# Five buffers of relus in place of six and twelve blocks in place of eleven, in a fused attention and expert layer

## The chip, the cores and the metric

The kernel runs on one core of a Trainium2 chip. Its engines are TensorE (PE: matmuls, with PEld for its weight loads), VectorE (DVE), ScalarE (ACT), GpSimd (POOL) and SyncE (SP, which here only starts DMAs). The metric is the device time of one execution in microseconds (us).

## What is computed

A layer over x of shape (4, 1024, 128): a normalisation, then power-law attention with 16 heads of width 8 and a mixture of 8 experts, of which each token uses two. The sum of both is added to x. All of it is in 32-bit floats.

```python
xn = _layernorm(x)
# attention, per head
q, k, v = split(xn @ W_attn + b_attn)
s = einsum('bhtd,bhsd->bhts', q, k)
s = s - s.mean(-1)
mad = abs(s).mean(-1) + 1e-06            # over all keys, before the causal mask
s = s / mad * score_gain
r = maximum(where(causal, s, -1000), 0) ** 4
y = (r / (r.sum(-1) + 1e-06)) @ v        # then @ W_proj + b_proj
# experts: top 2 of 8 by xn @ gate_w + gate_b, softmax over the two
h = (xn @ w1 + b1) * (xn @ w2 + b2)
e = silu(h @ wg + bg) @ w3 + b3
out = x + attention + sum of weighted e
```

## The kernel before

**Attention.** For each of the four batches, `prepare` makes queries, keys and values. The keys are written four times, each time masked to the heads of one of four groups (`keys`, L908), so that a matmul on 32 of PE's rows yields one head's scores, and four such matmuls run side by side. Queries, masked keys, transposed rows and normalised rows each lie in a buffer of kind `blk`.

`chunk` handles 512 queries of a batch; there are two chunks in a batch, four head groups r in a chunk. Two streams of steps run through it:

- "up" (L1010): scores of all keys, for the mean of their absolute values; ACT (L1025) or DVE (L1023) drains them.
- "score" (L1134): causal scores, keys on the partitions. A group is four heads by up to 512 queries, in four PSUM banks. DVE masks the diagonal part (L1153), and ACT (L1160) or DVE (L1162) takes the relu of the rest; both write two buffers of kind `u1`. Then ACT (L1185) or POOL (L1187) squares `u1` into a buffer of kind `u`, and squares `u` in place. The fourth powers times the values (L1210, `values`) and the plain relus times a constant (L1201, `relus`: the sum of absolute values that the relu gives) are added up in one PSUM bank.

There are 160 such groups. `flush` puts the values of one group and the relu sums of the next into one PE step, L1210 followed by L1201. At the end of a head group, `finish` turns the result and normalises it (L1078 to L1099); at the end of a chunk it is projected (L1267, L1269).

**Experts.** `route` finds places for the tokens; POOL scatters the rows to memory with 64 indirect DMAs (L776), from where 36 expert steps, each of two tiles of 128 rows, read them (L1303), with their weights (L1311 to L1314, eight DMAs a step on SP). Their matmuls are L1342, L1351 and L1360; POOL adds the results into memory with indirect DMAs (L1380).

**Order.** Nothing is ordered by hand. Each step is a `Node` with the engines that may do it, their durations, the nodes that it depends on, the buffers that it takes and gives back, and a rank. `Plan.run` goes through them once, at build time: again and again it takes the node whose start, less a lead from the table `SOONER`, is earliest, breaks ties by the rank (with an offset from the table `RANK`), puts it on that engine, and lets its buffers go or come free at planned times; `HOP` is the planned delay from a step's end to what depends on it. The program is issued in that order, so each engine's queue is fixed. On the chip an engine waits only for what its data and buffers need.

The buffers are counted in `kinds` (L245 to L253): 8 PSUM banks, 8 of `u`, 6 of `u1`, 11 of `blk`. A score takes four banks and two `u1`. A pair of `u1` is given back by a "free" node, which has no instruction:

```python
relu_job = dict(..., free=(u1s, e2), ...)          # L1219: e2, the second squares
...
add("free", {"none": 0.0}, None, deps=[n] + e2, give=u1s)   # L1063: n, the flush with the relu sums
```

A buffer of `u1` has 4096 bytes in each partition, one of `blk` 4160. PE also gets filler matmuls in planned gaps (L1531, L1536).

Of the kernel before, what the change touches and what calls it, by code (L numbers as in the profile page):

```python
# [16 lines left out]
P = 128  # L17
# [6 lines left out]
CH = 512  # L24
# [28 lines left out]
class Plan:  # L53

    HOP = 0.12
    LAG = {"PE": 0.2, "DVE": 0.085, "ACT": 0.1, "POOL": 0.045}

    SOONER = {"score": 0.46, "sum": -0.74, "mean": 0.17, "wT@DVE": 0.13, "norm@ACT": -0.05, "place": 0.03, "sums": 0.22, "relu0": -0.21, "relu2": -0.08, "score0": 0.74, "score2": 0.58, "sq2": 0.1, "ys0": -0.42, "out": -0.17, "v": -0.03, "gain": -0.81, "absq": 0.38, "abs0": -0.55, "sq0": -0.35, "proj": -0.44, "xT": 0.07, "second": -0.98, "up2": 0.18, "yT": 0.14, "up": 0.32, "sq@ACT": -0.27, "tbias": -0.01, "mask0": 0.04, "up0": 0.3, "abs0@DVE": 0.57, "ys2": -0.14, "ys@DVE": -0.79, "sq@POOL": -0.64, "weight": -0.19, "gate@ACT": -0.71, "count": 0.31, "k": 0.27, "turn": -0.06, "xT@ACT": 0.41, "y@DVE": 0.14, "gateT": 0.32, "abs2@DVE": 0.08, "gate": 0.05, "scatter": -0.07, "heads@ACT": 0.06, "abs@DVE": -0.3, "exp": 0.12, "xT@DVE": -0.16, "moments": -0.1, "keys": -0.69, "heads@DVE": 0.12, "relu0@ACT": -0.27, "rows": -0.52, "av0": -0.04, "scale": 0.09, "sq2@ACT": -0.42, "xg": -0.43, "av2": 0.03, "ys": 0.07, "abs2": 0.05, "warm": -0.75, "bias": -0.8, "gates": 0.91, "std": 0.14, "ys@ACT": -0.12, "sq0@ACT": -0.2, "q@ACT": 0.05, "ys2@ACT": -0.68, "mask": -0.04, "q": 0.08, "bound@DVE": -0.04, "norm": 0.17, "y": 0.11, "yT@DVE": -0.66, "norm@DVE": -0.66, "ys0@ACT": 0.07, "give": 0.2, "sq0@POOL": 0.01, "yT@ACT": -0.42, "headsT": 0.91, "abs2@ACT": -0.01, "blocks": -0.07, "sq": -0.1, "rows_in": -0.92, "xg@ACT": 0.35, "h": 0.17, "relu@DVE": -0.2, "load": 0.26, "xg@DVE": -0.07, "bound": 0.03, "abs": 0.51, "spill": -0.52, "kappa": 0.65, "relu2@DVE": -0.07, "relu": 0.05}  # L60
    RANK = {"xg": -16, "headsT": 6, "spill": 168, "blocks": 174, "wT": 8, "absq": 58, "abs": 20, "weight": 101, "gain": 188, "keys": -227, "abs2": 39, "sq2": 19, "ys0": -9, "up0": -37, "score2": 1, "av": -8, "second": 1, "score0": 14, "relu2": 94, "heads": -7, "norm": 28, "abs0": -107, "h": 174, "sums": 228, "av0": 17, "xT": -7, "relu": -11, "stats": -9, "rows_in": -149, "gateT": -21, "sq": 161, "top": 102, "reload": 84, "ys2": 27, "k": 242, "up": 10, "hot": -130, "score": -18, "sum": 13, "mean": 156, "kappa": -33, "load": -208, "warm": 37, "ys": -195, "yT": 1, "turn": -123, "rows": -17, "av2": 1, "out": 6, "normal": 62, "proj": -184, "scale": 29, "fill": 13, "mask2": 35, "sq0": -53, "tbias": -32, "count": 13, "gates": 7, "std": 24, "up2": -6, "gate": 6, "bias": 6, "mask0": -13, "v": 14, "scatter": 1, "g": 53, "moments": -184}
    MODE = {"up": "rows", "score": "rows", "av": "columns", "gate": "columns", "heads": "columns"}

    @classmethod
# [113 lines left out]
def layer_kernel(  # L178
# [44 lines left out]
    TB = T // P  # L223
# [8 lines left out]
    WX = C + 2  # L232
# [9 lines left out]
    def keep(shape, name, dtype=F32):  # L242
# [2 lines left out]

    kinds = {
        "bank": (8, [P, CH]),
        "u": (8, [P, 2, CH]), "u1": (6, [P, 2, CH]), "blk": (11, [P, TB * WX]),
        "w": (4, [P, 2 * F + FB * F + FB * C]), "xg": (3, [P, SB, WX]), "xT": (2, [P, TW]),
        "z": (2, [P, FB, TW]), "s": (2, [P, FB, TW]), "ye": (2, [P, SB, C]),         "ys": (2, [P, CH]), "yt": (2, [P, CB, C]),  # L250
        "yT": (1, [P, CH]), "wT": (2, [P, P]), "asum": (2, [P, 2, CB, NH]), "shead": (2, [P, TB, NH]),
# [8 lines left out]
    add = plan.add  # L260
# [11 lines left out]
    rows = keep([3, P], "rows")  # L272
# [8 lines left out]
    gain = keep([P, 1], "gain")  # L281
# [14 lines left out]
    for r in range(NR):  # L296
        for g in range(4):
            h = g * NR + r
# [20 lines left out]
    for base, step in ((0, -D), (D - 1, D)):  # L319
        nc.gpsimd.affine_select(  # L320
            out=same.rearrange("p (h d) -> p h d", d=D), in_=same.rearrange("p (h d) -> p h d", d=D),
# [7 lines left out]
        out=causal[:, : 2 * P].rearrange("p (n k) -> p n k", k=P), in_=causal[:, : 2 * P].rearrange("p (n k) -> p n k", k=P),  # L329
# [3 lines left out]
    for i in range(kinds["V"][0]):  # L333
        v = keep([P, TB, VW], f"V_{i}")
# [11 lines left out]
        out=behind_, in_=behind_, compare_op=ALU.is_ge, fill=0.0,  # L346
# [53 lines left out]
    none = tiles["w"][0][:, FILL * WX : FILL * WX + 2 * C]  # L400
# [43 lines left out]
    hot = [keep([P, E, NTB], f"hot_{k}") for k in range(2)]  # L444
# [350 lines left out]
    q, km, Vb, sh, prepared, keyed = {}, {}, {}, {}, {}, {}  # L795
# [190 lines left out]
    def chunk(b, c, vd, sh_done, t0, t1):  # L986
# [10 lines left out]
        for n, (r, unit) in enumerate(work):  # L997
# [20 lines left out]
            for g, k in enumerate(ks_):  # L1018
                def drain(e, r=r, parts=parts, g=g, k=k):
                    for i, sg, _, w, at in parts:  # L1020
# [9 lines left out]
                        deps=[a], behind=drained[0][:1], take=[] if drained[0] else [asum], give=[k], rank=rank - 200,  # L1030
# [15 lines left out]
        def flush(jobs, rank):  # L1046

            n = add(
                "av" + stage, {"PE": sum(o["took"] for o in jobs)}, lambda e: [o["emit"](e) for o in jobs],
                deps=[d for o in jobs for d in o["deps"]] + chain, take=[t for o in jobs for t in o["take"]],  # L1050
                give=[u for o in jobs for u in o["give"]], rank=rank - 20,
                behind=line["turn"][-2:-1] if any(o["take"] for o in jobs) else [],
            )
            chain[:] = [n]
            for o in jobs:
                if o["last"]:
                    n.closed = o["acc"]
                else:
                    n.open = o["acc"]
            for o in jobs:  # L1060
                if o["free"]:
                    u1s, e2 = o["free"]
                    add("free", {"none": 0.0}, None, deps=[n] + e2, give=u1s)  # L1063
                if o["last"]:
                    finish(*o["last"], n, rank)

# [46 lines left out]
        for r in range(NR):  # L1113
            acc = Buf("bank")
            for j, grp in enumerate(groups):
                diag = grp[0][0] >= c * CB
# [9 lines left out]
                e1, e2, sq1 = [], [], []  # L1126
                u1s, us = ([Buf(kind) for _ in range(2)] for kind in ("u1", "u"))
# [17 lines left out]
                for m in range(2):  # L1145
                    u1, u = u1s[m], us[m]
# [59 lines left out]
                def values(e, r=r, parts=parts, us=us, acc=acc, begin=False, end=False):  # L1206
# [362 lines left out]
```

## Time and profile before

| | us |
|---|---|
| median of 3 runs | 919.82 |
| lowest, highest | 916.57, 923.04 |
| profiled execution | 898.9 |
| its span, first to last instruction | 897.2 |
| granted TensorE clock, mean | 0.993 |

A table of busy time lists for each engine how long it was at work. A line of the groups names the line of the kernel, the engine, the operation, output and input, the count and the mean time of one. PE's matmuls overlap, so the time of a group of them is that of their union.

```profile
L1187 POOL TENSOR_TENSOR u<-u 128x1024 f32<-128x1024 f32 (+1 forms) x302 | 523.7, 1828 | 97.6 <-ACT u L1160 50.3
L1185 ACT ACTIVATE u<-u 128x1024 f32<-128x1024 f32 (+1 forms) x338 | 324.9, 991 | 7.0 <-DVE u L1162 3.1
L1025 ACT ACTIVATE bank<-bank 128x512 f32<-128x512 f32 (+3 forms) x351 | 170.6, 487 | 33.6 <-PE bank L1010 30.7
L1160 ACT ACTIVATE u<-bank 128x256 f32<-128x256 f32 (+2 forms) x353 | 152.9, 496 | 35.1 <-PE bank L1134 17.8
```

The 640 squares are shared by POOL (302, 1.83 us each on average) and ACT (338, 0.99 us). The last part of a line is the idle time of the engine just before such instructions, and what ended most of it: POOL stood idle for 97.6 us before squares, 50.3 us of it until ACT had written relus.

### The profile page before, as it was taken

The numbers are of one execution on the slowest core, as the hardware profiler recorded it, in microseconds if no ns is written. First come the engines' busy times: TensorE is split into PE (matmuls) and PEld (weight loads), VectorE is DVE, ScalarE is ACT, GpSimd is POOL, SyncE is SP. The second block draws the span as 40 slices with busy tenths as digits, with TensorE's granted clock in tenths as the row PEclk, the third lists the DMA queues.
The fourth block names the chain that finished last, engine by engine and source line by source line (L and its number), as shares of the span: only waits on it lengthen the run. The fifth ranks groups of instructions, "written<-read, shape, count | busy, mean of one in ns | idle before, by whom it ended". The sixth has DMA issues, their size and how long they took to land.

```text
span 897.2 us, 22584 instructions
## 1 busy us (share of the span) xinstructions
PE 878.7 (98%) x8067; PEld 472.7 (53%) x8067; DVE 592.8 (66%) x1557; ACT 787.4 (88%) x1881; POOL 709.8 (79%) x563
## 2 busy tenths in 40 slices
PE   7899999999999999999999999999999999999997
PEld 6455533334545555555566665555545666544444
DVE  6988967677875655655666576555756775755555
ACT  4978999999997999899988989989988978889995
POOL 4368999999996869787667839889787567599998
PEclk9989999999999999999999999999999999999999
DMA  4753000000001443535444534354213444422115
GB/s 112 289 160 100 25 26 28 32 16 25 23 22 35 108 130 85 134 74 138 99 107 108 136 85 129 85 132 116 71 49 75 103 107 107 111 72 53 24 14 187
DMA packets 92318, 79.20 MB, mean 88 GB/s; under 512 B 8431, under 2 KB 88366, under 8 KB 92206
## 3 DMA queue, kind: packets, MB, share of 16 engines
q1 hardware_dynamic: 79064, 68.50, 25.5%
q0 software_dynamic: 12416, 8.99, 7.1%
q8 instruction: 64, 1.05, 0.5%
q10 hardware_dynamic: 726, 0.27, 0.2%
q14 instruction: 48, 0.39, 0.1%
HBM read 58.13 MB, written 19.60 MB: 87 GB/s over the span
## 4 chain that ended last, share of the span: by engine, by line
PE 83%; ACT 6%; DVE 4%; POOL 4%; issue 2%; DMA 0%; ACTq 0%; DVEq 0%; POOLq 0%
PE bank L1010 16%; PE bank L1134 15%; PE bank L1210 14%; PE bank L1201 10%; PE bank L1351 7%; PE bank L1342 7%; PE bank L1360 4%; POOL u L1187 2%; ACT u L1185 2%; POOL xs L776 2%; PE bank L1078 1%; ACT u L1160 1%; PE bank L1531 1%; DVE asum L1023 1%; PE bank L826 1%
## 5 line engine op out<-in xcount | busy, mean ns | idle before, releaser
L1187 POOL TENSOR_TENSOR u<-u 128x1024 f32<-128x1024 f32 (+1 forms) x302 | 523.7, 1828 | 97.6 <-ACT u L1160 50.3
L1185 ACT ACTIVATE u<-u 128x1024 f32<-128x1024 f32 (+1 forms) x338 | 324.9, 991 | 7.0 <-DVE u L1162 3.1
L1023 DVE TENSOR_REDUCE asum<-bank 128x1 f32<-128x512 f32 (+3 forms) x417 | 203.1, 547 | 71.2 <-PE bank L1010 70.1
L1025 ACT ACTIVATE bank<-bank 128x512 f32<-128x512 f32 (+3 forms) x351 | 170.6, 487 | 33.6 <-PE bank L1010 30.7
L1160 ACT ACTIVATE u<-bank 128x256 f32<-128x256 f32 (+2 forms) x353 | 152.9, 496 | 35.1 <-PE bank L1134 17.8
L1010 PE MATMUL bank<-blk,blk 32*128 32x512 f32 (+3 forms) x1536 | 181.0, 523 | 1.6 <-ACT s L1452 1.5
L1134 PE MATMUL bank<-blk,blk 32*128 32x512 f32 (+3 forms) x1536 | 179.2, 529 | 1.2 <-ACT blk L908 0.7
L1153 DVE SCALAR_TENSOR_TENSOR u<-bank,causal 128x256 f32<-128x256 f32 (+1 forms) x384 | 121.2, 373 | 75.9 <-PE bank L1134 39.2
L1380 POOL DMA_INDIRECT acc<-ye,xg x72 | 113.4, 1574 | 66.5 <-DVE ye L1372 40.1
L1210 PE MATMUL bank<-u,V 128*32 128x512 f32 (+3 forms) x1536 | 159.5, 498 | 0.0
L1162 DVE TENSOR_SCALAR u<-bank 128x512 f32<-128x512 f32 (+1 forms) x159 | 99.3, 660 | 50.1 <-PE bank L1134 50.0
L1010 PEld LDWEIGHTS bank<-blk,blk 32*128 32x128 f32 x1536 | 87.3, 184 | 78.9 <-DVE asum L1023 14.8
L1201 PE MATMUL bank<-u,pick 128*32 128x512 f32 (+3 forms) x1280 | 125.4, 469 | 0.0
L1134 PEld LDWEIGHTS bank<-blk,blk 32*128 32x128 f32 x1536 | 65.9, 185 | 65.1 <-issue 26.1
L1201 PEld LDWEIGHTS bank<-u,pick 128*32 128x32 f32 x1280 | 42.2, 111 | 80.2 <-issue 75.6
L1210 PEld LDWEIGHTS bank<-u,V 128*32 128x32 f32 x1536 | 32.8, 108 | 88.3 <-issue 66.6
L1351 PEld LDWEIGHTS bank<-z,w 128*128 128x128 f32 x576 | 67.2, 192 | 18.4 <-issue 5.9
L1426 DVE SCALAR_TENSOR_TENSOR z<-bank,biases,z 128x128 f32<-128x128 f32 x144 | 43.6, 345 | 46.2 <-ACT z L1419 45.3
L1351 PE MATMUL bank<-z,w 128*128 128x128 f32 x576 | 73.3, 280 | 0.0
L776 POOL DMA_INDIRECT xs<-blk,slot x64 | 62.7, 979 | 13.5 <-issue 11.2
L1342 PE MATMUL bank<-xT,w 128*128 128x128 f32 x576 | 70.3, 275 | 0.0
L1025 ACT ACTIVATION_READ_ACCUMULATOR bank<-bank 128x1 f32 x351 | 68.1, 194 | 0.0
(191 smaller groups left out, 727.3 us busy)
## 6 DMA issues: line engine op xcount, KB each, us to landing
w<-in_L_ffn_w_dram SPq DMA_DIRECT2D x216, 128.0 KB
w<-in_L_ffn_wg_dram SPq DMA_DIRECT2D x72, 256.0 KB
xs<-w SPq DMA_DIRECT2D x1, 4680.0 KB
xg<-xs SPq DMA_DIRECT2D x36, 130.0 KB
acc<-w SPq DMA_DIRECT2D x1, 2048.0 KB
blk<-acc SPq DMA_DIRECT2D x4, 512.0 KB
out_dram<-xt SPq DMA_DIRECT2D x8, 256.0 KB
xt<-in_L_attn_x_dram SPq DMA_DIRECT2D x3, 512.0 KB
```

The source lines that it names most:

```text
L1010: nc.tensor.matmul(of_buf(ks_[g])[:, at : at + w], of_buf(q[b])[rows_, ii * P : (ii + 1) * P], of_buf(km[b][r])[rows_, k0 : k0 + w], start ...
L1023: nc.vector.tensor_reduce(to, of_, AX.X, ALU.add, apply_absolute_value=True)
L1025: nc.scalar.activation(of_, of_, AF.Abs, accum_out=to)
L1134: nc.tensor.matmul(of_buf(ks_[g])[:, at : at + n], of_buf(km[b][r])[rows_, jj * P : (jj + 1) * P], of_buf(q[b])[rows_, c * CH + off : (c + ...
L1153: nc.vector.scalar_tensor_tensor(of_buf(u1)[:, g, :near], of_buf(k)[:, :near], 0.0, allowed[:, :near], ALU.max, ALU.mult)
L1160: nc.scalar.activation(to, s_, AF.Relu)
L1185: nc.scalar.activation(to, s_, AF.Square)
L1187: (nc.vector if e == "DVE" else nc.gpsimd).tensor_tensor(to, s_, s_, ALU.mult)
L1201: nc.tensor.matmul(of_buf(acc)[32 * g : 32 * g + 32, off + lo : CH], pick, of_buf(u1s[g // 2])[:, g % 2, at + lo : at + n], start=begin, s ...
L1210: nc.tensor.matmul(of_buf(acc)[32 * g : 32 * g + 32, off:CH], of_buf(Vb[b])[:, jj, h0 : h0 + 32], of_buf(us[g // 2])[:, g % 2, at : at + n ...
L1342: nc.tensor.matmul(of_buf(k)[:, m * TW + j * TS : m * TW + (j + 1) * TS], weights_of(i, j)[m][:, f * P : (f + 1) * P], of_buf(tile_[i]["xT ...
L1351: nc.tensor.matmul(of_buf(k)[:, g * TW + j * TS : g * TW + (j + 1) * TS], weights_of(i, j)[2][:, f, g * P : (g + 1) * P], of_buf(tile_[i][ ...
```

## The change

The number of `u1` buffers goes from 6 to 5 and that of `blk` from 11 to 12. The "free" node of a pair of `u1` depends on the first squares (`sq1`) and no longer on the second (`e2`); it still depends on the flush with the relu sums. `HOP` goes from 0.12 to 0.14, and both tables, `SOONER` and `RANK`, are replaced as a whole. The diff, with the tables cut to some of their entries:

```diff
-    HOP = 0.12
+    HOP = 0.14
...
-    SOONER = {"score": 0.46, ..., "place": 0.03, ..., "sq@POOL": -0.64, ..., "keys": -0.69, ..., "rows_in": -0.92, ..., "load": 0.26, ..., "sq": -0.1, "second": -0.98, ...}
+    SOONER = {"score": 0.4, ..., "place": 1.09, ..., "sq@POOL": -0.21, ..., "keys": -1.37, ..., "rows_in": -0.04, ..., "load": -0.85, ..., "sq": -0.39, "second": 0.75, ...}
...
-    RANK = {"xg": -16, "headsT": 6, "spill": 168, ..., "keys": -227, ..., "relu": -11, ..., "sq": 161, ...}
+    RANK = {"xg": 24, "headsT": 15, "spill": -189, ..., "keys": 7, ..., "relu": -229, ..., "sq": -100, ...}
...
-        "u": (8, [P, 2, CH]), "u1": (6, [P, 2, CH]), "blk": (11, [P, TB * WX]),
+        "u": (8, [P, 2, CH]), "u1": (5, [P, 2, CH]), "blk": (12, [P, TB * WX]),
...
-                    u1s, e2 = o["free"]
-                    add("free", {"none": 0.0}, None, deps=[n] + e2, give=u1s)
+                    u1s, squared = o["free"]
+                    add("free", {"none": 0.0}, None, deps=[n] + squared, give=u1s)
...
-                    free=(u1s, e2), last=None, take=[acc] if begin and not diag else [],
+                    free=(u1s, sq1), last=None, take=[acc] if begin and not diag else [],
...
-                        add("free", {"none": 0.0}, None, deps=e2, give=u1s)
+                        add("free", {"none": 0.0}, None, deps=sq1, give=u1s)
```

More of the change, by code (lines that the diff above doesn't have):

```diff
@@ L53 @@
 class Plan:
-    HOP = 0.12
+    HOP = 0.14
     LAG = {"PE": 0.2, "DVE": 0.085, "ACT": 0.1, "POOL": 0.045}
-    SOONER = {"score": 0.46, "sum": -0.74, "mean": 0.17, "wT@DVE": 0.13, "norm@ACT": -0.05, "place": 0.03, "sums": 0.22, "relu0": -0.21, "relu2": -0.08, "score0": 0.74, "score2": 0.58, "sq2": 0.1, "ys0": -0.42, "out": -0.17, "v": -0.03, "gain": -0.81, "absq": 0.38, "abs0": -0.55, "sq0": -0.35, "proj": -0.44, "xT": 0.07, "second": -0.98, "up2": 0.18, "yT": 0.14, "up": 0.32, "sq@ACT": -0.27, "tbias": -0.01, "mask0": 0.04, "up0": 0.3, "abs0@DVE": 0.57, "ys2": -0.14, "ys@DVE": -0.79, "sq@POOL": -0.64, "weight": -0.19, "gate@ACT": -0.71, "count": 0.31, "k": 0.27, "turn": -0.06, "xT@ACT": 0.41, "y@DVE": 0.14, "gateT": 0.32, "abs2@DVE": 0.08, "gate": 0.05, "scatter": -0.07, "heads@ACT": 0.06, "abs@DVE": -0.3, "exp": 0.12, "xT@DVE": -0.16, "moments": -0.1, "keys": -0.69, "heads@DVE": 0.12, "relu0@ACT": -0.27, "rows": -0.52, "av0": -0.04, "scale": 0.09, "sq2@ACT": -0.42, "xg": -0.43, "av2": 0.03, "ys": 0.07, "abs2": 0.05, "warm": -0.75, "bias": -0.8, "gates": 0.91, "std": 0.14, "ys@ACT": -0.12, "sq0@ACT": -0.2, "q@ACT": 0.05, "ys2@ACT": -0.68, "mask": -0.04, "q": 0.08, "bound@DVE": -0.04, "norm": 0.17, "y": 0.11, "yT@DVE": -0.66, "norm@DVE": -0.66, "ys0@ACT": 0.07, "give": 0.2, "sq0@POOL": 0.01, "yT@ACT": -0.42, "headsT": 0.91, "abs2@ACT": -0.01, "blocks": -0.07, "sq": -0.1, "rows_in": -0.92, "xg@ACT": 0.35, "h": 0.17, "relu@DVE": -0.2, "load": 0.26, "xg@DVE": -0.07, "bound": 0.03, "abs": 0.51, "spill": -0.52, "kappa": 0.65, "relu2@DVE": -0.07, "relu": 0.05}
@@ L61 @@
-    RANK = {"xg": -16, "headsT": 6, "spill": 168, "blocks": 174, "wT": 8, "absq": 58, "abs": 20, "weight": 101, "gain": 188, "keys": -227, "abs2": 39, "sq2": 19, "ys0": -9, "up0": -37, "score2": 1, "av": -8, "second": 1, "score0": 14, "relu2": 94, "heads": -7, "norm": 28, "abs0": -107, "h": 174, "sums": 228, "av0": 17, "xT": -7, "relu": -11, "stats": -9, "rows_in": -149, "gateT": -21, "sq": 161, "top": 102, "reload": 84, "ys2": 27, "k": 242, "up": 10, "hot": -130, "score": -18, "sum": 13, "mean": 156, "kappa": -33, "load": -208, "warm": 37, "ys": -195, "yT": 1, "turn": -123, "rows": -17, "av2": 1, "out": 6, "normal": 62, "proj": -184, "scale": 29, "fill": 13, "mask2": 35, "sq0": -53, "tbias": -32, "count": 13, "gates": 7, "std": 24, "up2": -6, "gate": 6, "bias": 6, "mask0": -13, "v": 14, "scatter": 1, "g": 53, "moments": -184}
+    SOONER = {"score": 0.4, "sum": -0.7, "mean": -0.62, "wT@DVE": 0.25, "norm@ACT": 0.09, "place": 1.09, "sums": 0.12, "score0": 0.47, "score2": 0.47, "sq2": -0.22, "ys0": 0.03, "v": -0.2, "gain": -0.16, "absq": -0.04, "abs0": -0.32, "sq0": 0.1, "proj": -0.32, "second": 0.75, "up2": 0.03, "yT": 0.05, "up": 0.26, "sq@ACT": -0.31, "tbias": 0.31, "mask0": 0.33, "up0": 0.34, "abs0@DVE": 0.62, "ys@DVE": 0.23, "sq@POOL": -0.21, "gate@ACT": -0.31, "xT@ACT": 0.19, "y@DVE": 0.17, "gateT": 0.01, "gate": -0.75, "heads@ACT": -0.42, "abs@DVE": -0.09, "keys": -1.37, "heads@DVE": 0.02, "rows": 0.51, "scale": -0.35, "sq2@ACT": -0.24, "xg": -0.13, "ys": 0.22, "abs2": 0.05, "warm": -0.03, "std": 0.67, "ys2@ACT": 0.02, "mask": 0.17, "q": -0.15, "bound@DVE": 0.18, "norm": -0.34, "yT@DVE": -0.63, "ys0@ACT": 0.5, "sq0@POOL": 0.12, "yT@ACT": -0.59, "headsT": -0.17, "abs2@ACT": -0.3, "blocks": 1.53, "sq": -0.39, "rows_in": -0.04, "h": 0.08, "relu@DVE": -0.02, "load": -0.85, "bound": 0.75, "abs": -0.04, "kappa": 0.77, "relu": -0.47, "abs@ACT": -0.42, "sq2@POOL": -0.6, "ys2@DVE": -0.1, "relu0@DVE": -0.31, "top": 0.12, "q@DVE": -0.02, "abs0@ACT": 0.32, "normal": -0.14, "relu@ACT": 0.44, "wT": -0.44, "y@ACT": 0.05, "bound@ACT": -0.03, "g": -0.07, "ys0@DVE": 0.02, "av": 0.17, "reload": 0.64, "wT@ACT": -0.19, "hot": -0.16, "mask2": -0.05, "stats": 1.6}
@@ new lines @@
+    RANK = {"xg": 24, "headsT": 15, "spill": -189, "blocks": 11, "wT": -3, "absq": -27, "abs": -233, "weight": 75, "gain": -16, "keys": 7, "abs2": -31, "sq2": -158, "up0": 23, "score2": 52, "av": -26, "second": -168, "score0": 238, "heads": -23, "norm": 132, "abs0": -74, "h": 25, "sums": -52, "av0": -16, "relu": -229, "stats": -138, "rows_in": 11, "gateT": 11, "sq": -100, "reload": 29, "k": -36, "hot": -106, "score": -7, "sum": 16, "mean": -190, "kappa": 35, "warm": 8, "ys": -6, "yT": 206, "turn": 30, "av2": -25, "out": -19, "normal": -3, "proj": 55, "scale": 123, "fill": -5, "mask2": 187, "sq0": -25, "tbias": 41, "count": 89, "gates": -13, "up2": 99, "mask0": 116, "v": 4, "g": 159, "moments": -18, "give": 30, "q": -78, "exp": 19, "place": -6, "y": -36, "bound": 5}
```

## The prediction

> **What bounds the kernel now.** I read the page's busy shares first, then busy time by stretch, then TensorE's timeline, and last the lines that feed it.
>
> ```profile
> PE 878.7 (98%) x8067; PEld 472.7 (53%) x8067; DVE 592.8 (66%) x1557; ACT 787.4 (88%) x1881; POOL 709.8 (79%) x563
> ...
> PE 83%; ACT 6%; DVE 4%; POOL 4%; issue 2%; DMA 0%; ACTq 0%; DVEq 0%; POOLq 0%
> ```
>
> PE is the busiest engine and carries the chain of waits. A busy PE can still be slow inside its work, so I split its time: each matmul record of a 512-column step streams 0.427 us (a quarter of it when four 32-row or 32-column matmuls share the array), which sums to 713 us over all records, 16 of them the kernel's own filler matmuls. Changes between the three array layouts recur with fixed sizes (a score followed by values loses 0.218 us, a relu sum followed by a score 0.119); 862 changes make some 126 us. What is left, 58 us, is real stalling: 43 us of it lies before 300 us, 15 us behind. The busy times by stretch show why:
>
> ```profile
> 100.00:200.00 100.00, 99.91 (x864) 38.46 (x856) 74.16 (x171) 94.50 (x175) 91.66 (x108) 1.00 0.08 27
> ...
> 300.00:875.00 575.00, 573.26 (x5398) 319.37 (x5392) 351.70 (x911) 518.97 (x1280) 452.37 (x273) 1.00 0.39 94
> ```
>
> (Columns: stretch, its length, busy PE, PEld, DVE, ACT, POOL.) Until the experts' matmuls arrive at about 250 us, ACT (94.5 of 100) and POOL (91.7 of 100) set the pace by their squares. From 300 us on PE alone does, 573.26 of 575, with nearly nothing to win.
>
> **The change part by part.** It removes no instruction and adds none. It has four edits.
>
> *Six relu buffers become five.* A score takes two at once and they come back two at once, so five hold two groups, as four would; six hold three. I counted, at the start of each of the 160 scores, how many groups (that one included) had not begun their relu sums: 3 for 69 scores, 2 for 82, 1 for 9. Those 69 scores (43%) must move behind a step that they now precede. Averaged from 50 to 870 us, 2.43 pairs are out; at most 2 will be.
>
> What a move costs is read from the place where one happens:
>
> ```profile
> 404.77 1.14 PE L1134 MATMUL bank<-blk,blk 32*128 32x512 f32 x8
> 405.84 1.16 PE L1360 MATMUL bank<-w,s 128*128 128x128 f32 x8
> 406.84 1.95 PE L1342 MATMUL bank<-xT,w 128*128 128x128 f32 x16
> 408.72 1.14 PE L1134 MATMUL bank<-blk,blk 32*128 32x512 f32 x8
> 409.79 1.07 PE L1210 MATMUL bank<-u,V 128*32 128x128 f32 x16
> 410.68 0.40 PE L1201 MATMUL bank<-u,pick 128*32 128x128 f32 x8
> ```
>
> The score at 408.72 is a third group. It has to follow the values and relu sums at 409.79 and 410.68, which last to 411.01: a swap of 1.07 us with 1.22 us. PE loses nothing if those can go first; the relus that wait for the score (L1160 on ACT, L1162 on DVE, both in order, with absolute sums L1025 and L1023 and squares queued behind) come about 1.2 us later.
>
> Can the values and relu sums go first? They need the second squares of the group before. Following each square to its group (the squares of POOL and of ACT come in the program's order), a group's second squares end 9.0 us after its score starts (mean), its relu sums end after 12.6 us. So for group k the step was ready 6.0 us (mean) before score k+2 started. With 2.2 us allowed for the step itself and the hop, 128 of 156 scores need no delay at all. The other 28 need 30.9 us together: 21.7 us for 19 scores before 250 us, 9.3 us for 9 after it. Both are bounds from above, since other matmuls can be put in between. Below, the cost is nothing, and a gain isn't excluded, as squares queue less. Before 250 us PE has the slack (43 us of stalls, 16 of filler), so a late score costs only what ACT and POOL then lack to do. I take 0.3 of both, some 9 us, as ACT and POOL at 92 to 95% have little time to be left idle, but a backlog of squares (up to four groups in the eight "u" buffers) to be fed from.
>
> *Given back with the first squares.* It helps less than it sounds: a pair is still held until its relu sums, and those end last in 118 of 160 groups. Mean holding time falls from 12.98 to 12.65 us, mean occupancy from 2.43 to 2.37 pairs. So 0.3 us per group comes back: it cannot make up for the third pair.
>
> *A twelfth block.* It is worth what waits for a block. The 16 key masks are the likely ones:
>
> ```profile
> L908 ACT ACTIVATE blk<-blk,cstat,rmask x16: 1227/1229/1247, 30.1 to 717.0; 128x1024 f32<-128x1024 f32 x16
> ...
> its engine sat idle before it (us, times) until:
> who waited for it (us, times):
>   PEld bank L1134: 1.5, 1
>   PEld bank L1360: 0.8, 1
>   PE bank L1134: 0.7, 1
> ```
>
> ACT never stood idle before one; 0.7 us of PE waited for one (the first score), and there the scaled queries (L876 on DVE) ended at 32.39 us, later than the key mask at 31.34. Counting holders: at 437 us, where the third batch is prepared, the batch before holds its queries and one key block (the other three were last read at 353, 370 and 401 us), the new one three and three more: 8 of 11. At 219 us it is 10. Only between about 22 and 34 us do all 11 fill (four of rows, three transposed for the spill, queries, keys). The reload of transposed rows, an SP issue (0.33 to 0.41 us each, three in all), could come before the loads queued around it; it stands at 410 us for a batch whose projections start at 420, and at 49 us for one that starts at 199, so nothing is won. Gain: 0 to 1 us.
>
> *A new table of leads and ranks, and a hop of 0.14.* This reorders everything: first squares lean more to POOL than before, routing ("place") and "second" come sooner, expert loads (eight issues on SP a time) 1.1 us later in the planner's eyes, "rows_in" sooner. Loads are hidden now: weights have four buffers, so a pair of them loads while another is used (issues from 404.39 to 410.3 us in the timeline); with that cover gone a load that is 1.1 us late would cost up to 1.1 us in each of 36 expert steps, 40 us in all. For the rest the trace shows no new order; its size is bounded by what an order can waste or save: 43 us of stalls plus 16 us of filler before 300 us, of which ACT and POOL forbid most, and 15 us later. I take 0, with 10 us either way.
>
> Sum: 9 - 1 + 0, some 8 us less what reordering takes back; I take 5. The profiled execution has a span of 897.2 us and 898.9 in all, so 904. The median of the runs shown is 919.82, 2.3% above that execution; nothing in the trace explains the difference, so I add the same 5 us there: 925.
>
> **A rule against it.** The trace has one clear price of a PE stall:
>
> ```profile
> 279.79 1.57 PE L1010 MATMUL bank<-blk,blk 32*128 32x512 f32 x14
> 282.90 0.69 PE L1010 MATMUL bank<-blk,blk 32*128 32x256 f32 x2 [1.55 <-ACT s L1452]
> 283.53 1.52 PE L1210 MATMUL bank<-u,V 128*32 128x512 f32 x8
> 284.80 2.38 PE L1201 MATMUL bank<-u,pick 128*32 128x384 f32 x16
> ...
> 284.00:290.00 6.00, 6.00 (x47) 2.95 (x40) 1.62 (x4) 2.11 (x9) 0.00 (x0) 0.72 0.01 3
> ```
>
> After an idle 1.55 us the granted clock is 0.72 over the next 6 us: half speed for 3.4 us, a loss of 1.7 us on top of the stall. (A like stretch, 6.8 us long, follows 62 us.) The Trainium skill, "TensorE: Matmul & The Clock Gate", Part 1, has the clock fall only after an idle window of about 3.4 us. By the page, the 28 delayed scores, none over 3.2 us, would cost no clock; by the trace each stall of 1.5 us costs 1.7 more. The measurement decides: if six of them bite, 10 us are added to my 5. That is not in the likeliest sum, and is in the range. The same skill ("Perfetto Trace Analysis", Optimization Strategy) reads a gap that keeps recurring as a sign of too few buffers. No such gap recurs after 300 us here; if the changed profile shows one, the relu buffers are the suspects.
>
> **The rivals.**
> - *A wash.* Two groups suffice: the ready step (6.0 us early on average) simply goes first. -1 to +9 us, 919 to 929 as the sum, 911 to 929 with the new order's luck. For it: 573.26 of 575. Chance 0.43, the likeliest; its number 925.
> - *Starved squares (the slower side).* Before 250 us, squares on ACT and POOL run out of relus because the third group may not start; the place is the wait of L1187 on POOL for L1160 and L1162. If all 30.9 us pass through, with six clock drops (10 us), it is 961; with half of the delays and one drop or two, 938. It decides once more than 9 of the 31 us reach ACT and POOL. Against it: the delays are short and few; for it: both at over 90% there, and three groups out in half of the time (51%). A layout change is also lost where a score no longer stands beside another 32-row step: 0.1 us in each of 69 moves, 7 us. Chance 0.41, 929 to 955.
> - *The new order is better.* If a quarter of the 59 us of stalls and filler before 300 us goes, 15 us: 905. For it: routing is led sooner, and the experts' matmuls that fill PE could start before 248 us. Against: squares are conserved, and ACT and POOL have 5 to 8% left there. Chance 0.16, 897 to 911.
> - *It does less than it says:* the fifth relu buffer and the twelfth block both lie unused. That is inside the wash.
>
> **How the numbers follow.** About 1%, 9 us, is what a measurement here can tell from no change (the runs shown spread over 6.5 us). Faster by more: 0.16; within: 0.43; slower by more: 0.41. As both signs hold much of the chance, the wash's own range is 911 to 929. The range for all cuts some 0.1 at either end: 907 to 947. Predicted: 925.
>
> **What would show it.** Right: at most 2 groups out at any score; stalls after 300 us still under 20 us; before 300 us somewhat more PE stalls, or over the run more POOL waits on L1160 and L1162 than now (72.0 us); key masks no earlier in any way that a score feels. Wrong: POOL or ACT busier than 95% between 100 and 250 us and experts' rows read before 240 us (then it is faster), or PE's layout changes well over 862 and half-clock stretches more than two (then it is slower).

## The result, and the profile after

| | before | changed |
|---|---|---|
| median of 4 runs, us | 921.43 | 944.59 |
| lowest, highest, us | 916.57, 923.46 | 942.55, 945.73 |
| profiled execution, us | 898.9 | 942.55 |
| its span, us | 897.2 | 940.8 |
| granted TensorE clock, mean | 0.993 | 0.975 |

The ratio is 1.0257, with a 95% interval from 1.0208 to 1.0306: 23 us slower. The kernel before took 921 to 925 us (medians) in three sets of runs, each set on one chip, and 897 to 898 us in three other sets; its profiled execution belongs with the second kind, the runs of the verdict with the first. So the pair 897.2 and 940.8 overstates the change.

First the page of the changed kernel: the busy time of all engines, then PE and the granted clock in 40 slices (tenths), then the shares of the chain of waits.

```profile
PE 903.8 (96%) x8103; PEld 475.1 (50%) x8103; DVE 602.7 (64%) x1580; ACT 771.3 (82%) x1812; POOL 733.7 (78%) x574
...
PE   7999899999589999999999999999999999999997
...
PEclk9989999999579999999999999999999999999999
...
PE 86%; ACT 5%; DVE 3%; another core or an unknown queue 2%; POOL 2%; issue 1%; DMA 0%; ACTq 0%; DVEq 0%; POOLq 0%
```

PE is still the bound, but in the eleventh slice (235 to 259 us) it is busy for half of the time, and the clock falls there and after it. The same kernel in a set in which the kernel before took 898 us (the run "after_again" below) shows no such slice:

```profile
PE 886.4 (98%) x8103; PEld 469.2 (52%) x8103; DVE 601.9 (67%) x1580; ACT 770.9 (85%) x1812; POOL 733.4 (81%) x574
...
PE   7999999999999999999999999999999999999997
...
PEclk9999999999999999999999999999999999999999
```

Busy time by stretch, which carried the prediction, first of the changed kernel's profile, then of "after_again" (columns: stretch, its length, busy PE, PEld, DVE, ACT, POOL, clock):

```profile
100.00:200.00 100.00, 96.33 (x835) 37.08 (x831) 70.09 (x165) 80.82 (x162) 87.33 (x83) 0.98 0.06 18
300.00:875.00 575.00, 572.04 (x5370) 316.31 (x5359) 354.66 (x916) 499.54 (x1217) 475.90 (x289) 1.00 0.38 94
```

```profile
100.00:200.00 100.00, 99.31 (x882) 36.88 (x874) 72.99 (x173) 83.99 (x154) 93.66 (x81) 1.00 0.05 15
300.00:875.00 575.00, 572.04 (x5349) 313.77 (x5349) 353.55 (x916) 502.72 (x1213) 470.81 (x284) 1.00 0.37 93
```

From 300 us on nothing is lost in either. Whatever the 37 us between these two profiles of one program are, they lie before 300 us.

PE's time can be split as in the prediction (streaming, filler, changes, stalls). All in us, from the profiled execution of each; 2 to 3 us at the ends are in no column:

| kernel | span | streaming | filler | changes (their number) | stalls | of these before 300 us |
|---|---|---|---|---|---|---|
| before | 897.2 | 696.1 | 15.7 | 125.9 (862) | 57.5 | 42.6 |
| changed, "after_again" | 903.6 | 696.2 | 24.2 | 134.7 (906) | 46.2 | 29.5 |
| before, "again" | 922.9 | 696.3 | 15.8 | 126.1 (864) | 83.0 | 63.7 |
| changed, verdict | 940.8 | 696.0 | 24.0 | 134.7 (906) | 82.8 | 64.0 |

One name has to be put right. The prediction called its 862 changes "changes between the three array layouts", but they are all the places where PE goes from the matmuls of one line to those of another. Of the 862, 578 change the layout; the rest do not (141 are values followed by relu sums). Of the 906, 628 do.

Filler and changes belong to the program and are the same wherever it runs: +8.5 and +8.8 us for the change. The stalls are not. In the upper pair the changed kernel has 11.3 us fewer of them, and the net is +6.4 us. In the lower pair its stalls are as long as those of the kernel before: under those conditions the change loses the 11 us that it had won. Filler stands only where the plan leaves PE a gap, so part of the stalls has only changed its name: filler and stalls together, the time in which PE has no work, are 73.2 and 70.4 us in the upper pair. The net of +6.4 us there is the 8.8 us of changes, less these 2.8, and 0.4 of the rest.

*Where the extra stalls are.* The kernel's planner leaves a planned start for each step; before ends its plan at 892.2 us, the changed kernel at 904.4. The start of each score in the trace, less its planned start, is a drift that shows at which moment time is lost:

| drift, us, at about | 50 us | 80 | 105 to 115 | 222 to 233 | 275 to 286 | end |
|---|---|---|---|---|---|---|
| changed, "after_again" | 0.1 | 2.3 | 1.6 | 1.1 | 0.1 | 0.4 |
| changed, verdict | 0.9 | 4.7 | 13.3 | 12.7 | 37.2 | 37.2 |

8.6 us are lost between 80 and 115 us, 24.5 between 233 and 286, and little elsewhere. In these two places POOL issues scatters (L776) in long runs, with no square between them: 5 (from 76.5 us) and 10 (from 98.1 us) of the 64 in the first, 24 in the second. Busy time in the second, of the verdict's profile (scatters from 230.7 to 261.4 us) and then of "after_again" (from 219.1 to 251.6 us):

```profile
225.00:231.00 6.00, 5.95 (x44) 2.69 (x39) 4.84 (x14) 5.77 (x10) 5.52 (x8) 1.00 0.08 25
...
238.00:245.00 7.00, 3.50 (x16) 1.65 (x16) 0.87 (x4) 1.85 (x4) 5.45 (x12) 0.54 0.14 48
245.00:252.00 7.00, 4.09 (x9) 1.72 (x10) 1.69 (x4) 1.04 (x3) 5.68 (x13) 0.50 0.16 54
252.00:262.00 10.00, 6.35 (x8) 1.49 (x6) 1.21 (x3) 0.61 (x2) 7.91 (x15) 0.50 0.15 49
```

```profile
238.00:245.00 7.00, 7.00 (x62) 2.75 (x61) 5.22 (x9) 7.00 (x16) 5.90 (x11) 1.00 0.17 57
245.00:252.00 7.00, 6.99 (x92) 3.23 (x91) 5.16 (x16) 6.86 (x15) 5.86 (x12) 1.00 0.16 50
252.00:262.00 10.00, 10.00 (x83) 4.93 (x82) 9.09 (x26) 8.01 (x24) 8.12 (x5) 1.00 0.56 168
```

Between 238 and 252 us, in which POOL issues scatters in both, ACT works 2.9 of 14 us in the first and 13.9 in the second; PE runs 25 matmuls against 154. Only POOL keeps its pace (11.1 and 11.8 us), and the data moved per second (the last column, GB/s) are alike. PE's timeline of the verdict's profile (start, duration, work, and in brackets the idle time before it with what ended it) and POOL's:

```profile
236.03 0.49 PE L1134 MATMUL bank<-blk,blk 32*128 32x128 f32 x4
239.77 2.08 PE L1134 MATMUL bank<-blk,blk 32*128 32x128 f32 x12 [3.26 <-issue]
241.23 2.05 PE L1010 MATMUL bank<-blk,blk 32*128 32x512 f32 x4
245.56 2.08 PE L1010 MATMUL bank<-blk,blk 32*128 32x512 f32 x4 [2.28 <-DVE V L947]
249.99 1.11 PE L1078 MATMUL bank<-ident,ys 128*128 128x128 f32 x4 [2.35 <-ACT u L1160]
```

```profile
237.09 0.97 POOL L776 DMA_INDIRECT xs<-blk,slot  x1 [0.22 <-issue]
238.06 0.09 POOL L775 MEMSET scrap<- 1x1 f32 x1
238.37 0.97 POOL L776 DMA_INDIRECT xs<-blk,slot  x1 [0.22 <-issue]
239.34 0.09 POOL L775 MEMSET scrap<- 1x1 f32 x1
239.65 0.97 POOL L776 DMA_INDIRECT xs<-blk,slot  x1 [0.22 <-issue]
```

A score of sixteen matmuls is broken in the middle: four, then 3.26 us in which PE waits for nothing that the profile shows ("issue"), then twelve. The later waits are for DVE and ACT, which do next to nothing themselves in this time. This is no starving of squares: POOL's queue holds nothing but scatters, their memsets and one copy here, and a score whose first four matmuls could run stops short. Nor do the instructions take longer once they run. Two of them, on DVE and on ACT, in the same profile:

```profile
249.09 0.42 DVE L1153 SCALAR_TENSOR_TENSOR u<-bank,causal 128x256 f32<-128x256 f32 x1 [3.59 <-PE bank L1010]
...
254.07 0.38 ACT L1160 ACTIVATE u<-bank 128x256 f32<-128x256 f32 x1 [2.44 <-PE bank L1010]
```

Outside the standstill the same two take 0.41 and 0.38 us (medians of 252 and 113). Only their starts are late, and the statement above that an engine waits only for its data and buffers does not account for that. The engines do not wait for their program either: no packet of an instruction queue moves from 227 to 263 us, and the next that brings PE's instructions comes at the same place of its program as in "after_again" (after 3762 and 3766 of PE's matmuls, weight loads and waits). Such stretches are called standstills below.

### The profile page after: what moved, and what is told of

Read it like the earlier page. It is cut to its first block, busy times and chain, and to the rows that moved or that the text cites. A ratio compares the mean times of both kernels' runs of the same rounds, so it can differ in the third digit from the quotient of the medians.

```text
span 940.8 us, 22563 instructions
## 1 busy us (share of the span) xinstructions
PE 903.8 (96%) x8103; PEld 475.1 (50%) x8103; DVE 602.7 (64%) x1580; ACT 771.3 (82%) x1812; POOL 733.7 (78%) x574
## 3 DMA queue, kind: packets, MB, share of 16 engines
q1 hardware_dynamic: 79064, 68.50, 24.5%
q8 instruction: 64, 1.05, 0.5%
## 4 chain that ended last, share of the span: by engine, by line
PE 86%; ACT 5%; DVE 3%; another core or an unknown queue 2%; POOL 2%; issue 1%; DMA 0%; ACTq 0%; DVEq 0%; POOLq 0%
PE bank L1134 17%; PE bank L1010 16%; PE bank L1210 14%; PE bank L1201 10%; PE bank L1351 7%; PE bank L1342 7%; PE bank L1360 4%; PE bank L1536 2%; PE bank L1078 2%; ACT u L1185 1%; POOL u L1187 1%; PE bank L826 1%; ACT bank L1025 1%; ACT u L1160 1%
## 5 line engine op out<-in xcount | busy, mean ns | idle before, releaser
L1187 POOL TENSOR_TENSOR u<-u 128x1024 f32<-128x1024 f32 (+1 forms) x313 | 539.4, 1787 | 149.9 <-ACT u L1160 51.1
L1185 ACT ACTIVATE u<-u 128x1024 f32<-128x1024 f32 (+1 forms) x327 | 314.0, 982 | 20.1 <-DVE u L1153 16.9
L1023 DVE TENSOR_REDUCE asum<-bank 128x1 f32<-128x512 f32 (+3 forms) x452 | 221.0, 543 | 111.4 <-PE bank L1010 93.9
L1160 ACT ACTIVATE u<-bank 128x384 f32<-128x384 f32 (+2 forms) x385 | 170.5, 506 | 73.8 <-PE bank L1134 36.9
L1010 PE MATMUL bank<-blk,blk 32*128 32x512 f32 (+3 forms) x1536 | 191.8, 532 | 7.1 <-DVE asum L1023 3.6
L1134 PE MATMUL bank<-blk,blk 32*128 32x512 f32 (+3 forms) x1536 | 181.6, 534 | 6.6 <-issue 3.3
L1025 ACT ACTIVATE bank<-bank 128x512 f32<-128x512 f32 (+3 forms) x316 | 155.0, 492 | 33.3 <-PE bank L1010 21.3
L1153 DVE SCALAR_TENSOR_TENSOR u<-bank,causal 128x256 f32<-128x256 f32 (+1 forms) x384 | 120.8, 372 | 64.7 <-PE bank L1134 32.3
L1010 PEld LDWEIGHTS bank<-blk,blk 32*128 32x128 f32 x1536 | 83.8, 187 | 92.4 <-issue 19.8
L1162 DVE TENSOR_SCALAR u<-bank 128x512 f32<-128x512 f32 (+2 forms) x127 | 77.9, 644 | 46.2 <-PE bank L1134 45.3
L1134 PEld LDWEIGHTS bank<-blk,blk 32*128 32x128 f32 x1536 | 66.2, 186 | 64.8 <-issue 34.3
L1210 PEld LDWEIGHTS bank<-u,V 128*32 128x32 f32 x1536 | 33.3, 108 | 97.2 <-issue 66.6
L1351 PE MATMUL bank<-z,w 128*128 128x128 f32 x576 | 73.2, 280 | 0.0
L776 POOL DMA_INDIRECT xs<-blk,slot x64 | 62.7, 980 | 13.3 <-issue 12.9
L1342 PEld LDWEIGHTS bank<-xT,w 128*128 128x128 f32 x576 | 67.2, 192 | 0.8 <-ACT u L1160 0.8
```

The costliest lines, as they stand in the source:

```text
L1010: nc.tensor.matmul(of_buf(ks_[g])[:, at : at + w], of_buf(q[b])[rows_, ii * P : (ii + 1) * P], of_buf(km[b][r])[rows_, k0 : k0 + w], start ...
L1023: nc.vector.tensor_reduce(to, of_, AX.X, ALU.add, apply_absolute_value=True)
L1025: nc.scalar.activation(of_, of_, AF.Abs, accum_out=to)
L1134: nc.tensor.matmul(of_buf(ks_[g])[:, at : at + n], of_buf(km[b][r])[rows_, jj * P : (jj + 1) * P], of_buf(q[b])[rows_, c * CH + off : (c + ...
L1153: nc.vector.scalar_tensor_tensor(of_buf(u1)[:, g, :near], of_buf(k)[:, :near], 0.0, allowed[:, :near], ALU.max, ALU.mult)
L1160: nc.scalar.activation(to, s_, AF.Relu)
```

## The experiments

Theory A: the standstills beside long runs of scatters are what separates the two kernels beyond the planned order. Rivals: two pairs of relu buffers starve the squares (the prediction's slower side); the new tables are at fault; POOL is simply held too long. Runs of one set share the runs of the kernel before on the same chip.

**The kernel before once more** ("again", no edit).

> The kernel before, once more, for a second trace of it. Theory A (a freeze): in the changed kernel's trace ScalarE, VectorE and TensorE stand nearly still from 235 to 265 us, while GpSimd issues 24 scatters in a row, and this costs about 25 us against the order that the planner laid out. The kernel before has runs of at most 8 scatters, so its trace should keep within 10 us of the planner's times and end near 900 us, or, if the 916 to 923 us of its timed runs come from the same cause, show one such standstill of about 20 us near 236 to 246 us. Theory B (starved by two groups alone): no standstill in it, and the time near 920 us is spread over the whole run.

924.57 us, span 922.9, beside 924.87 for the other runs of this set. Here the drift rises from 0.6 to 10.2 us by 106 us, 15.0 by 131, 16.1 by 231, 20.8 by 257, 29.1 by 284, 33.3 by 317, and ends at 31.9. So the kernel before has standstills too, beside its own runs of scatters (8, 6, 6 and 8; a run of 4 from 124 us makes none), 25.7 us more of span than in its first profile. (The 3.4 us before 317 us are no standstill: its first profile has them too.) PE's timeline at the first run:

```profile
80.96 0.38 PE L1210 MATMUL bank<-u,V 128*32 128x128 f32 x2 [0.43 <-issue]
82.38 0.38 PE L1210 MATMUL bank<-u,V 128*32 128x128 f32 x3 [1.05 <-issue]
83.14 0.27 PE L1210 MATMUL bank<-u,V 128*32 128x128 f32 x1 [0.38 <-issue]
```

The matmuls of one step come in ones, twos and threes, with idle time put down to "issue" before each. In the changed kernel the standstills cost 940.8 - 903.6 = 37.2 us, here 25.7: the change makes them 11.5 us longer, which with the 6.4 us of the order gives 17.9, the distance of the two spans. The next run finds 17.7 within one set; the verdict's 23.2 has 5 us more, by which the sets of this kind differ (921.43 and 924.87 before, 944.59 changed and 942.58 for the same order in "four_eleven") and which no trace settles.

**Four relu buffers and eleven blocks** ("four_eleven").

```diff
-        "u": (8, [P, 2, CH]), "u1": (5, [P, 2, CH]), "blk": (12, [P, TB * WX]),
+        "u": (8, [P, 2, CH]), "u1": (4, [P, 2, CH]), "blk": (11, [P, TB * WX]),
```

> The changed kernel with four relu buffers in place of five and eleven blocks in place of twelve. If the fifth buffer and the twelfth block are never needed, the order of steps is the same and the time is that of the changed kernel, 944.6 us, within 3 us (2.5% above before). If either is of use, it is slower by over 5 us.

942.58 us, ratio 1.021 [1.017, 1.025] to the kernel before in its set: the changed kernel's time. The planner gives the same order. The fifth relu buffer and the twelfth block are not used at all; what the change does is to go from three pairs to two, to give them back sooner, and to reorder.

**Scatters a little later** ("late_scatters").

```diff
-    SOONER = {"score": 0.4,
+    SOONER = {"scatter": -0.3, "score": 0.4,
...
```

> The changed kernel with one entry more in the table of leads, scatter -0.3: the order is new, the planner's own end is 922.5 us in place of 904.4, and the longest run of scatters on GpSimd has 7 in place of 24. Theory A (a freeze in long runs of scatters): no standstill near 240 us, so the span stays about 7 us above the planner's end, some 930 us, 12 us faster than the changed kernel. Theory B (the planned order and the two groups cost the time): 18 us slower than the changed kernel, about 960 us.

939.51 us, ratio 1.0163 [1.0129, 1.0197]; 930 was expected. No run of scatters has more than 7 now, and the plan is 18 us longer (922.5), yet the time does not rise above that of "four_eleven" in the same set (3 us less, with single runs that overlap): in the profiled execution, the slowest of the four, the drift ends at 18.9 us in place of some 36. Shorter runs stand still less; the expectation that runs of 7 would be free was wrong.

**The old tables and hop, with the rest of the change** ("old_tables"): `SOONER` and `RANK` too are those of before.

```diff
-    HOP = 0.14
+    HOP = 0.12
...
```

> The changed kernel with the tables and the hop of before: five relu buffers given back with the first squares, twelve blocks. The planner's own end is 930.3 us, 38 above that of before; the longest run of scatters has 4. Theory A: span some 7 us above that, 937 us, so 5 us faster than the changed kernel, though the tables don't suit. Theory B: the two groups cost their full 38 us, 958 us, as no standstill explains the changed kernel's time.

938.58 us, ratio 1.0155 [1.0117, 1.0193]. Its plan is the longer one (930.3 us), and its span of 936.2 is only 5.9 above it, in a set where the kernel before ends with a drift of 31.9. Its scatters never stand more than four in a row; POOL's timeline shows squares among them:

```profile
70.47 0.97 POOL L776 DMA_INDIRECT xs<-blk,slot  x1 [0.21 <-issue]
71.47 1.91 POOL L1187 TENSOR_TENSOR u<-u 128x1024 f32<-128x1024 f32 x1
73.31 0.09 POOL L775 MEMSET scrap<- 1x1 f32 x1
73.57 0.99 POOL L776 DMA_INDIRECT xs<-blk,slot  x1 [0.17 <-issue]
74.56 0.09 POOL L775 MEMSET scrap<- 1x1 f32 x1
74.86 0.96 POOL L776 DMA_INDIRECT xs<-blk,slot  x1 [0.21 <-issue]
75.85 1.90 POOL L1187 TENSOR_TENSOR u<-u 128x1024 f32<-128x1024 f32 x1
```

It is not wholly free of standstills. The drift goes from 2.5 us at 85 us to 7.5 at 106, and beside the one run of four in this time (from 97.8 us) a score is broken off after six matmuls:

```profile
102.08 0.71 PE L1134 MATMUL bank<-blk,blk 32*128 32x256 f32 x6
104.44 0.69 PE L1134 MATMUL bank<-blk,blk 32*128 32x256 f32 x2 [1.65 <-DVE asum L1023]
```

With at most these 5 us of standstill in it, two pairs under the old tables cost 936.2 - 897.2 = 39.0 us: 20.3 of filler (36.0), 11.4 of changes (137.3, 924 of them) and 6.8 of stalls (64.3). The two plans differ by 38.1.

**Scatters left out, POOL's time kept** ("plain_after", "plain_before"), on the changed kernel and on that before. The rows that the experts read stay empty.

```diff
-                    nc.gpsimd.memset(scrap, 0.0)
-                    d = nc.gpsimd.indirect_dma_start(
...
-                    apart(d, m)
+                    for _ in range(14):
+                        nc.gpsimd.memset(scrap, 0.0)
```

> The changed kernel with every one of its 64 scatters of token rows left out (nothing is written to the expert slots): in the place of each, POOL runs 14 tiny memsets, about 1.3 us, so that the planned order and POOL's time stay as they were. Theory A (the indirect transfers that POOL issues back to back make the other engines stand still): the drift against the planned starts stays at 5 to 13 us to the end, the time is 904.4 + 4 to 13 + 2 = 910 to 919 us. Rival B (POOL is simply held too long by a run of 24 pieces, and the squares queued behind them starve the PE, whatever the pieces are): nothing changes, 939 to 946 us.

> The kernel before, its 64 scatters left out and replaced by memsets in the same way. Theory A: 892.2 + 4 to 10 + 2 = 898 to 905 us, so that the two kernels without scatters differ by their planned ends, 12 us (8 to 16), and the rest of the 23 us between them as they stand is more standstill. Rival B: 919 to 927 us, and the difference to the changed kernel without scatters stays 18 to 24 us.

950.77 and 943.85 us, where the kernel before took 897.91: neither theory's number. The fault was in the experiment. Fourteen memsets took 2.0 us, a scatter with its memset 1.27, so POOL had 64 x 0.73 = 47 us more to do, and the time of both kernels rose by about 46 (943.85 against 897.91; 950.77 against the 905.08 of "after_again"). That says something else: while tokens are routed, POOL's time is on the path one for one. It says nothing about standstills, which this set did not have.

**All scatters in one run** ("early_scatters").

```diff
-    SOONER = {"score": 0.4,
+    SOONER = {"scatter": 1.0, "score": 0.4,
...
```

> The changed kernel with the due time of the scatters moved so far ahead that all 64 stand in one run on POOL; planned end 939.2 us against 904.4. Theory A, with about 1 us of standstill for each scatter of a long run (24.5 us in a run of 24): 1 x 64 = 55 to 70 us over the planned end, 995 to 1015 us. Rival B (POOL held, which the plan already counts): 943 to 955 us.

933.67 us, below its plan of 939.2. In a set where the kernel before takes 898 us, 64 scatters in a row make no standstill. So scatters alone do not make one; something that differs between the sets has to be there too.

**Given back with the second squares** ("second_squares").

```diff
-                    free=(u1s, sq1), last=None, take=[acc] if begin and not diag else [],
+                    free=(u1s, e2), last=None, take=[acc] if begin and not diag else [],
...
-                        add("free", {"none": 0.0}, None, deps=sq1, give=u1s)
+                        add("free", {"none": 0.0}, None, deps=e2, give=u1s)
```

> The changed kernel with the relu buffers given back with the second squares, as before. Planned end 917.8 us (13.4 above the changed kernel), runs of 5, 10, 4 and 21 scatters. If plan and standstills add up: 917.8 + 8.6 + 21 to 25 + 7 = 952 to 962 us, and giving back early is worth 10 to 16 us. If the give-back is worth what the prediction said (0.3 us at each of 55 scores at most, in no waiting of the PE): 943 to 948 us.

918.33 us (plan 917.8) in the same set: no standstill beside a run of 21 scatters, so the sum with standstills missed, while the early give-back is worth 918.33 - 905.08 = 13.3 us under like conditions (898 for the kernel before in both sets), as in the plans (13.4).

**The changed kernel once more** ("after_again", no edit).

> The changed kernel itself, once more. The kernel before took 924.87 us on one chip and 897.91 us on another, where no standstill was seen beside the scatters. Theory A2 (the standstills belong to some chips; the planned order does the rest): where the kernel before takes about 898 us, the changed one takes 904.4 + 4 to 8 = 908 to 912 us, ratio 1.011 to 1.016; where it takes 921 to 926 us, the changed one takes 941 to 946 us. Rival (the whole difference of 23 us is in the change and not in the chip): ratio 1.023 to 1.028 on either.

905.08 us beside 898.27: ratio 1.009 [1.0063, 1.0118], 6.8 us. The verdict's 23 us are not a property of the two programs alone. The time is nearly that of its plan (904.4), a little under what was expected, because the drift is 0.4 us where the kernel before has 6.

**Scatters left out, 9 memsets for each** ("plain9_after", "plain9_before", and "no_scatters", which is "plain9_after" once more).

```diff
-                    for _ in range(14):
+                    for _ in range(9):
```

> The changed kernel with its 64 scatters left out (the expert slots stay empty), 9 tiny memsets in the place of each instead of 14: the 14 took 2.0 us where a scatter with its memset takes 1.27 us, so that POOL was 46 us longer in the first 300 us and the time went up by the same. 9 x 0.142 = 1.28 us. Theory A2 on a chip with standstills: 906 to 918 us where the changed kernel takes 941 to 946; on a chip without: within 6 us of the changed kernel. Rival B (POOL held, whatever by): within 6 us of the changed kernel on either chip.

> The kernel before with its 64 scatters left out (the expert slots stay empty) and 9 tiny memsets on POOL in the place of each, 9 x 0.142 = 1.28 us. Where the kernel before itself takes about 898 us here: 892.2 + 4 to 8 = 894 to 902 us, within 5 us of it, and some 7 us (3 to 12) below the changed kernel without its scatters (906.96). Where the kernel before takes 921 to 926 us here: 896 to 908 us if the indirect transfers make the standstills (theory A2), 918 to 927 us if these have another cause.

> The changed kernel without its 64 scatters (9 tiny memsets for each, the expert slots stay empty), a second time, for a chip on which the kernel before shows the standstills. Where the kernel before takes 921 to 926 us here: 904 to 918 us if the indirect transfers make the standstills, 938 to 946 us, as the changed kernel itself, if they have another cause. Where the kernel before takes about 898 us: 905 to 909 us again, and the cause stays untried.

| run | us | before in its set | ratio |
|---|---|---|---|
| plain9_after | 906.96 | 898.27 | 1.011 [1.0076, 1.0143] |
| plain9_before | 898.26 | 896.91 | 1.0004 [0.9993, 1.0016] |
| no_scatters | 908.34 | 921.70 | 0.9846 [0.9826, 0.9865] |

The first two show that the substitute is now of the right length: without standstills the kernels take the same time with memsets as with scatters. The third is the test. In a set where the kernel before takes 921.70 us, the changed kernel without its scatters takes 908.34; with them it took 942.58 and 944.59 in the other two sets of that kind. 34 to 36 us go with the indirect transfers, though POOL is held as long. Busy time of "no_scatters" in the stretch of before:

```profile
238.00:245.00 7.00, 7.00 (x60) 3.21 (x59) 5.17 (x10) 7.00 (x17) 4.27 (x48) 1.00 0.00 0
245.00:252.00 7.00, 7.00 (x94) 3.33 (x86) 5.67 (x15) 7.00 (x15) 4.24 (x48) 1.00 0.01 4
252.00:262.00 10.00, 10.00 (x95) 4.76 (x88) 7.99 (x20) 8.85 (x24) 7.88 (x9) 1.00 0.01 2
```

PE and ACT are full again. That POOL is held is refuted as the cause; that there is no standstill without the indirect transfers is shown, in the one set of this kind in which they were left out.

What differs between the sets is not known, but their traces differ in one more thing. A scatter lands with 16 semaphore updates. Of the 1024 updates of the 64 scatters, the profiles of the kind with standstills hold 458 to 591, those of the other kind 1016 to 1024. For the first kind the profile therefore has no time of landing. The line of the scatters between 225 and 270 us, of the verdict's profile and then of "after_again" (the last number, where there is one, is the us from issue to landing):

```profile
xs<-blk,slot POOLq DMA_INDIRECT x26
```

```profile
xs<-blk,slot POOLq DMA_INDIRECT x20, 2.3
```

In "no_scatters" too some updates of later loads are missing (4546 on record, 5010 in "plain9_after"). The steps that wait for these updates ran, so it is the records that are missing. Each execution here has a recorded span and clock. Whether the recording takes part in the standstills, and whether an execution that is not recorded has any, is a rival that no run tries.

Not tried: six relu buffers together with any other edit, since the planner then comes to a point where no step can go on, and the room does not hold six with twelve blocks. So the tables' gain is measured only with two pairs. The order of before with its scatters spread to shorter runs, which might win some of the 26 us that it loses in such sets, wasn't run either. No kernel that did the whole work was faster than the one before.

## Why the prediction was right, and where it was wrong

The time, 944.59 us, lies in the range (907 to 947), near its end. The likeliest case, a wash at 925, did not come about in the verdict's runs; the number came out where the slower rival stood (929 to 955), but not by its mechanism. In the other kind of set the difference is 6.8 us, inside the -1 to +9 us of the wash.

- *At most two groups out:* right. At the starts of the 160 scores 2 are out at 106 and 1 at 54 (before 3 at 69, 2 at 82, 1 at 9).
- *Five buffers, "some 9 us":* mis-sized by four times. With the old tables they cost 39.0 us, early give-back included. I counted when relu sums would be ready, 30.9 us of delay, and took 0.3 of it. More came from what two pairs do to the order: 62 more changes (59 of them of the layout), and gaps that the planner pads with filler. I had written down a layout price of 7 us (in the rival) and left it out of the sum; it measured 8.8 us in the changed kernel, more than the whole net.
- *Early give-back, 0.3 us a group:* the holding time may be right, its worth was not. It is 13.3 us, though it makes up for the third pair only in part.
- *A twelfth block, 0 to 1 us:* right, 0; it is unused.
- *New tables, "I take 0, with 10 us either way":* wrong in size. They are worth 936.2 - 903.6 = 32.6 us, up to 5 of it standstill in "old_tables" (25.9 by the two plans). Together with the buffers' 39.0 the net is +6.4 us of span; my sum was +5. That it fits is two errors of about 30 us that cancel.
- *The scatters:* the step that failed. No term of the sum prices the run lengths of scatters on POOL; the bound for the new order was "43 us of stalls plus 16 us of filler", read from a profile that had no standstills. The 11.5 us by which the changed runs of scatters (10 and 24 in place of 8 at most) lengthen them are in no case of mine. The sign stood in the data: the median was 2.3% above the profiled execution, and I wrote "nothing in the trace explains the difference, so I add the same 5 us there". A difference of 21 us that the trace does not contain was a cost that the change could touch.
- *The starved squares:* not seen. POOL's waits before squares, in "after_again" (engine, what waited for what: us in total, times, longest):

```profile
POOL u L1187 <- ACT u L1160: 50.5, 31, 19.2
POOL u L1187 <- DVE u L1153: 35.1, 19, 3.0
...
POOL u L1187 <- DVE u L1162: 9.6, 9, 1.8
```

For L1160 and L1162 together they fell from 72.0 to 60.1 us; those for the masked part (L1153) rose from 13.7 to 35.1. Longer waits of POOL came with fewer stalls of PE (46.2 against 57.5), so they cost nothing that can be seen.
- *The better order, 0.16:* its mechanism was a third there. Its 15 us were to come from stalls and filler before 300 us. The stalls there fell by 13.1 us (42.6 to 29.5), but filler took 8 of this back, so the two together fell by 5, from 58 to 53 us, and the changes took 8.8. The filler (L1536) in the profile of before and in that of "after_again" (minimum, median and maximum ns, first and last start, then the shapes):

```profile
L1536 PE MATMUL bank<-b3p,zeros x24: 275/486/697, 43.5 to 223.2; 128*128 128x384 f32 x14, 128*128 128x256 f32 x4, 128*128 128x128 f32 x4, 128*128 128x512 f32 x2
```

```profile
L1536 PE MATMUL bank<-b3p,zeros x50: 274/486/985, 39.3 to 665.0; 128*128 128x384 f32 x22, 128*128 128x256 f32 x18, 128*128 128x512 f32 x6, 128*128 128x128 f32 x4
```

- *The clock rule against the row:* the row (half speed after 1.55 us of idling) gave 10 us to the range. In the verdict's profile six idle times of PE, from 1.29 to 3.26 us, one after another, go with one stretch of 30.7 us at half clock. The table in the Trainium skill, "TensorE: Matmul & The Clock Gate", Part 1, asks for an idle window of about 3.4 us, and none reached it, so the row still stands against the table. (The same part also tells of a kernel whose clock went down and up again because PE idled briefly and often, which is nearer to this one.) But in "after_again", where PE never idles for more than 1.05 us from 30 us on, half speed lasts 3.4 us before the end. And in "old_tables" the score that was broken off for 1.65 us is followed by full speed (1.00 from 103 to 110 us). So the row is one case and no rule: the length of one idle time does not decide. The clock follows the standstills, and is a part of their 37 us, not a cost of the 28 delayed scores.
- *The signs:* of those for "slower", both came true in the verdict's profile (906 changes, only 5% over 862; four half-clock stretches before the end). The first holds in "after_again" too, where the change costs 6.8 us. Of those for "right", stalls after 300 us stayed under 20 (18.8), and the key masks made no score wait anew (PE waited 1.2 us for them in all, 0.7 before). "More stalls before 300 us" held only with the standstills.

## What to carry to other kernels

When the median stands 2% above the one execution that was profiled, profile again before pricing a change: the missing time has a place, and a change may lengthen it. A change of buffer counts in a planned kernel is two changes, what the count forbids and what the new order makes of it, and each should be run alone, since here some +39 and -33 us hid behind a net of 6. Time an order with long runs of indirect transfers on one queue in more than one set of runs: breaking them up halved what the standstills cost here (18.9 in place of 36 us), but the plan became 18 us longer, so nothing clear was won.

## What was not expected of the hardware

- In the sets of runs in which the kernel before takes 921 to 925 us, while POOL issued indirect transfers at its usual 0.96 us each and one every 1.3 us, PE, ACT and DVE nearly stopped: about 1 us lost for each of the 24 in the longest run. Where the kernel before takes 897 to 898 us the changed kernel lost nothing, and an order with 64 in a row neither. Two of the sets name the same chip number, with 924.87 and 896.91 us for the kernel before. Whether it is the chip, its neighbours, the moment or the recording is open, and so is the path by which the transfers hold up the other engines: the transfers' own rate and their time on POOL look alike in both kinds, and so do the times of the instructions that are late to start.
- Where no standstill occurs, the spans of before, "after_again", "second_squares" and "early_scatters" lie within 8 us of their planned ends of 892.2 to 939.2 us, the second and third within 1.5 us.
- POOL's time in the routing stretch is on the path: 47 us more of it made both kernels 46 us longer.
